# Moving a tile's scatter to the next tile's last unit, and a first exponential ahead of the loop

## The chip, the cores and the metric

The kernel runs on one core of a Trainium2 chip. The time is device microseconds of one launch. The engines are named as the profile names them: PE is TensorE (PEld its weight loads), DVE is VectorE, ACT is ScalarE, POOL is GpSimd, SP is SyncE. Each engine works through its own instructions in order; engines wait for each other by semaphores. A DMA is issued by the queue of one engine and carried out by 16 DMA engines that the core has.

## What is computed

One layer of graph attention over 3327 nodes with 1024 features each, with a residual:

```python
h = jnp.maximum(_layernorm(x, axis=-1), 0.0)
f = h @ Wf + bf
g = h @ Wg + bg
e = jax.nn.relu(f @ g.T)
scores = jnp.where(adj > 0, e, NEG)
attention = jax.nn.softmax(scores, axis=1)
out = x + attention @ (h @ W + bW)
```

The adjacency matrix `adj` (3327 x 3327, int32) is symmetric, has ones on its diagonal and few others: each row has some 17 neighbours on average. Rows of `attention` are zero away from those neighbours.

## The kernel before

The kernel uses that sparsity. A dense path (lines 38 to 292) stands ready for other inputs and is not run here. `edge_path` (from line 296) has two stages.

**First stage** (lines 354 to 671, up to about 250 us). It runs over 26 tiles of 128 rows. For each tile SP loads the adjacency rows `r` (line 410) and the rows of x (412); ScalarE turns the adjacency into 0 and 1 and counts them (420); POOL multiplies by the column number (427); VectorE takes the largest eight of each of 16 segments (478) and from these the list of the row's neighbours. Beside it x is normalised: mean and variance on VectorE for odd tiles (436) and on ScalarE for even ones (450, 453), a square root on ScalarE (446, 454), a reciprocal on VectorE (458), then scale and relu on ScalarE (463, 464). The normalised rows go to a table `hd` in HBM (466), the candidates to `cd` (471), the lists to `pd` (508). TensorE meanwhile transposes rows of Wg and Wf (534), ScalarE copies them out of PSUM (535), and TensorE multiplies them to one matrix A (554, 558), so that a score is h A h' plus a bias term. It also counts by degree (498, 503, with VectorE at 500), from which the nodes are sorted into 26 tiles of falling degree: `perm`.

**Edge stage** (from line 674). A tile s now holds 128 nodes of about the same degree; `CAPS[s]` says how many neighbours its nodes may have (37 for the first, 11 for the last). `ORDER` begins with tile 24, then 0 to 23, then 25. For a tile:

- `fetch` gathers by indirect DMA its lists `pi` and its own rows (744, 746; all gathers are issued at line 691 by POOL).
- `prepare` transposes the rows (703, 704) and multiplies them by A (764); `emptied` copies the result q out of PSUM (780) and refills the bank with the bias (727).
- `dots` gathers, for each neighbour k, 128 rows of `hd` into a buffer G (821; 26 buffers) and takes their dot products with q on VectorE (824).
- `softmax` (853 to 873) masks the scores, takes their maximum, and has ScalarE's exponential (860).
- `combine` sums the G rows by their weights. Some are scaled on ScalarE (904) and summed in PSUM by transposing matmuls (887), the others are added on VectorE (910).
- `project` multiplies the sum by W (918, 924). `result` copies it to a tile `res` (942; two buffers) and adds the rows of x to it by an accumulating gather (949).
- `finish` scatters `res` to the rows of the output (954). It is issued after the last gather traced so far (953).

A tile with more than 16 neighbours is split into two units, each with its own dots, softmax and combine; the others are one unit. Tiles 0 to 14 have two. The loop at line 1003 runs over the units. In a unit it fetches the tile after next (if the unit is its tile's last), takes the dots of the unit, its softmax, the first three dots of the next unit (`AHEAD`), finishes a waiting scatter (1013), combines, and in a tile's last unit issues the result of the tile before (1021) and prepares the tile after next.

What is traced in this order is then placed by a scheduler, which plans each engine's order from its own estimate of the durations. `in_line` and `tc.issue_after` tie single instructions to others. So a line moved or added can change the planned order elsewhere.

Of the kernel before, what the change touches and what calls it, by code (L numbers as in the profile page):

```python
# [8 lines left out]
FP = mybir.dt.float32  # L9
I32 = mybir.dt.int32  # L10
AF = mybir.ActivationFunctionType
# [284 lines left out]
def edge_path(ctx: ExitStack, tc: tile.TileContext, x, adj, Wf, bf, Wg, bg, W, bW, out, flag):  # L296
# [11 lines left out]
    nc = tc.nc  # L308
    N, D = x.shape
    O = W.shape[1]  # L310
    P = 128
# [26 lines left out]
    ident = const.tile([P, P], FP, name="ident")  # L338
# [345 lines left out]
    small = ctx.enter_context(tc.tile_pool(name="small", bufs=2))  # L684
# [36 lines left out]
    def filled(pool, name, row, w, at):  # L721
        ps = pool.tile([P, CB], FP, name=name)
        if at < 2:
            nc.tensor.matmul(ps, ident, A_sb[:, 0, :CB], start=True, stop=True)
        o = at * w % row.shape[1]
        banks[name, at] = ps
        return nc.scalar.copy(ps[:, :w], row[:, o : o + w])

    for at in range(2):
        filled(p_q, "ps_q", vb, QB, at)  # L730
        filled(p_o, "ps_o", bWb, CB, at)

    def fetch(s):

        if s == ORDER[1]:

            with tc.issue_after(st["gathered"].ins):
                return fetched(s)
        fetched(s)
# [8 lines left out]
    def prepare(s):  # L748
        e = st[s]
        pi = e["pi"]  # L750
        hT = hTpool.tile([P, KD, P], FP, name="hT")
        with in_line():
            copied, ins = transposed2(hT, e["hp"])
        if queue:
            queue["act"], queue["pe"] = copied, ins
        e["q"] = qpool.tile([P, QW], FP, name="q")
        e["ps_q"] = []
        for i, o in enumerate(range(0, QW, QB)):
            at = 3 * ORDER.index(s) + i
            ps = banks.pop(("ps_q", at))  # L760
            e["ps_q"].append(ps)
            with in_line():
                for k in range(KD):
                    ins = nc.tensor.matmul(  # L764
                        ps[:, :QB], hT[:, k, :], A_sb[:, k, o : o + QB], start=False, stop=(k == KD - 1),
                        skip_group_check=True,
                    )
            if queue:
                queue["pe"] = ins

            if not i:
                emptied(s, i)
        if not queue:
            prepared(s)
# [74 lines left out]
    def softmax(s, k0, k1, last):  # L849

        e = st[s]
        sc = e["sc"][:, k0:k1]
        nc.vector.scalar_tensor_tensor(sc, sc, 0.0, e["mask"][:, k0:k1], op0=ALU.max, op1=ALU.add)
        nm = small.tile([P, 1], FP, name="nm")
        nc.vector.tensor_reduce(nm, sc, AX.X, ALU.max, negate=True)
        if k0:
            nc.vector.tensor_tensor(nm, nm, e["nm"], op=ALU.min)  # L857
        l = small.tile([P, 1], FP, name="l")
        with in_line():
            nc.scalar.activation(sc, sc, AF.Exp, bias=nm, accum_out=l)  # L860
        if k0:
            al = small.tile([P, 1], FP, name="al")
            nc.scalar.activation(al, e["nm"], AF.Exp, bias=nm, scale=-1.0)
            nc.vector.scalar_tensor_tensor(l, e["l"], al, l, op0=ALU.mult, op1=ALU.add)
        if last:
            rs = small.tile([P, 1], FP, name="rs")
            nc.vector.reciprocal(rs, l)
            if k0:
                nc.vector.tensor_tensor(al, al, rs, op=ALU.mult)
            nc.vector.tensor_scalar(sc, sc, rs, None, op0=ALU.mult)  # L870
        if k0:
            queue["act"] = nc.scalar.activation(e["y"], e["y"], AF.Copy, scale=al)
        e["nm"], e["l"] = nm, l
# [19 lines left out]
    def combine(s, k0, k1, last):  # L893
        e = st[s]
        if not k0:
            e["y"] = G[s, 0]
        y = e["y"]
        e["first"] = True
        pe = on_tensor(s, k0, k1) if last else []
        for k in range(k0, k1):  # L900
            p = e["sc"][:, k : k + 1]
            g = G[s, k]
            if k in pe:
                queue["act"] = nc.scalar.activation(g, g, AF.Copy, scale=p)  # L904
                queue["pe"] = sum_transposed(e, g, e["first"], False)
                e["first"] = False
            elif k == 0:
                queue["act"] = nc.scalar.activation(y, y, AF.Copy, scale=p)  # L908
            else:
                e["summed"] = nc.vector.scalar_tensor_tensor(y, g, p, y, op0=ALU.mult, op1=ALU.add)  # L910

    def project(s):
        e = st[s]
        yT = yTpool.tile([P, KD, P], FP, name="yT")
        with in_line():
            queue["pe"] = sum_transposed(e, e["y"], e["first"], True)
            for g in range(0, KD, 4):
                queue["act"] = nc.scalar.copy(yT[:, g : g + 4, :], e["yT"][:, g : g + 4, :])  # L918
        e["o"] = []
        for o in range(OH):  # L920
            ps = banks.pop(("ps_o", OH * ORDER.index(s) + o))
            with in_line():
                for k in range(KD):
                    ins = nc.tensor.matmul(  # L924
                        ps, yT[:, k, :], W_sb[:, k, o * CB : (o + 1) * CB], start=False, stop=(k == KD - 1),
                        skip_group_check=True,
                    )
            e["o"].append(ps)
            queue["pe"] = ins

    def result(s):

        e = st[s]
        r = e["r"] = xpool.tile([P, O], FP, name="res")
        for o in range(OH):
            to, ps = r[:, o * CB : (o + 1) * CB], e["o"][o]
            if s == NT - 1:
                nc.vector.tensor_tensor(to, ps, e["x"][:, o * CB : (o + 1) * CB], op=ALU.add)
                continue
            at = OH * ORDER.index(s) + o + 2  # L940
            with in_line():
                ins = nc.scalar.copy(to, ps)  # L942
                if at < OH * NT:
                    ins = filled(p_o, "ps_o", bWb, CB, at)
            queue["act"] = ins


        if s < NT - 1:
            gather(r, x[:, :], perm[:, s : s + 1], compute_op=ALU.add)

    def finish(s):

        with tc.issue_after(st["gathered"].ins):
            ins = nc.gpsimd.indirect_dma_start(  # L954
                out=out[:, :],
                out_offset=bass.IndirectOffsetOnAxis(ap=perm[:, s : s + 1] if s < N // P else final, axis=0),
                in_=st[s]["r"],
                in_offset=None,
                bounds_check=None if s < N // P else N - 1,
                oob_is_err=s < N // P,  # L960
            )
        tc.declare_no_dep(ins.ins, group="results", reason="other rows")
        tc.add_to_no_dep_group("results", ins.ins)
# [19 lines left out]
    def dots(s, ks):  # L983
        for k in ks:
            if (s, k) not in done:
                done.add((s, k))

                dot(s, k, st[ORDER[-2]].get("summed") if s == ORDER[-1] else None)
# [13 lines left out]
    rest, done_with = None, []  # L1002
    for i, (s, k0, k1) in enumerate(units):
        last = k1 == CAPS[s]
        at = ORDER.index(s)
        if last and at + 2 < NT:
            fetch(ORDER[at + 2])
        dots(s, range(k0, k1))
        softmax(s, k0, k1, last)
        if i + 1 < len(units):  # L1010
            s2, a, b = units[i + 1]
            dots(s2, range(a, min(b, a + AHEAD)))
        if done_with:
            finish(done_with.pop())
        combine(s, k0, k1, last)
        if rest:
            rest()
            rest = None
        if last:
            if at:  # L1020
                result(ORDER[at - 1])
                done_with.append(ORDER[at - 1])
            if at + 2 < NT:
                prepare(ORDER[at + 2])

            def rest(s=s, at=at):
                if at + 2 < NT:
                    prepared(ORDER[at + 2])
                project(s)

            if not at or i + 1 == len(units) or units[i + 1][2] == CAPS[units[i + 1][0]]:
                rest()
                rest = None
            if at + 2 == NT - 1:
                bad = failed()
# [43 lines left out]
```

## Time and profile before

| | us |
|---|---|
| median of 7 runs | 1327.37 |
| lowest and highest of them | 1325.80, 1328.97 |
| profiled execution | 1324.11 |
| its span | 1322.4 |
| POOL, indirect DMA to G at line 691, 454 of them | 535.2 busy |
| VectorE, dots at line 824, 456 of them | 584.7 busy |
| VectorE, sums at line 910, 279 of them | 357.8 busy |
| TensorE, line 924, 832 matmuls | 365.7 busy |
| TensorE, line 764, 1248 matmuls | 368.0 busy |
| POOL idle ahead of the scatters at line 954 | 58.0 for res from DMA |

A row of a timeline below reads: start in us, duration in us, engine, line, operation, what is written from what, count, and in brackets the idle time of that engine just before it and what ended it. A row of waits reads: engine, what was to run, its line, whom it waited for, then us in all, times, and the longest. A row of windows has, for each stretch, the busy us of PE, PEld, DVE, ACT and POOL (instructions in parentheses), then TensorE's granted clock as a share of the full one, the busy share of the 16 DMA engines, and the GB/s.

### The profile page before, as it was taken

How to read it: one execution, taken by the hardware profiler on the slowest of the kernel's cores; microseconds unless marked ns; L12 is line 12 of the kernel's file. 1: busy time of each engine (PE TensorE's matmuls, PEld its weight loads, DVE VectorE, ACT ScalarE, POOL GpSimd, SP SyncE). 2: the span in 40 equal slices, each digit the busy share in tenths (PEclk: the TensorE clock that was granted, in tenths of full speed). 3: DMA queues.
4: the chain of work that ended last, by engine and by line, in shares of the span. 5: the costliest groups of instructions: out<-in, count | busy, mean ns of one | idle time of the engine just before them, and what ended most of it. 6: DMA issues, size and time to landing. Idle time of an engine off the chain costs nothing.

```text
span 1322.4 us, 14333 instructions
## 1 busy us (share of the span) xinstructions
PE 1113.7 (84%) x4448; PEld 706.3 (53%) x4448; DVE 1165.3 (88%) x2360; ACT 597.8 (45%) x940; POOL 896.2 (68%) x678
## 2 busy tenths in 40 slices
PE   2589797289329689899999998999999999999995
PEld 2355564156126547665666664666665555555553
DVE  4779899759977888999999999999989999999980
ACT  6779787214034525453454454334443333333350
POOL 6689889275556667777776777766666777776611
PEclk9999798589759899899999999999999999999998
DMA  9999996698458788889889889988887988888821
GB/s 351 338 368 355 386 370 243 233 320 321 152 182 307 271 298 266 297 308 309 312 294 313 313 307 320 306 263 300 279 287 245 294 284 289 275 270 281 285 85 50
DMA packets 101660, 374.46 MB, mean 283 GB/s; under 512 B 14731, under 2 KB 18474, under 8 KB 98247
## 3 DMA queue, kind: packets, MB, share of 16 engines
q0 software_dynamic: 79584, 286.77, 64.3%
q1 hardware_dynamic: 11004, 71.01, 14.0%
q10 hardware_dynamic: 10986, 15.67, 3.3%
q8 instruction: 37, 0.61, 0.2%
q14 instruction: 49, 0.40, 0.1%
HBM read 344.11 MB, written 29.30 MB: 282 GB/s over the span
## 4 chain that ended last, share of the span: by engine, by line
PE 35%; DVE 22%; issue 15%; ACT 10%; DMA 10%; POOL 7%; POOLq 0%; ACTq 0%; SPq 0%; DVEq 0%
PE ps_o L924 16%; PE ps_q L764 12%; DVE G L910 8%; ACT G L904 6%; DVE junk L824 6%; DMA G<-hd,pi 4%; DVE cand L478 4%; PE ps_A L554 4%; POOL G L691 3%; PE yT_ps L887 3%; POOL r L427 2%; DMA cd<-cand 1%; DMA res<-in_x_dram,perm 1%; ACT r L420 1%; DVE sc L824 1%
## 5 line engine op out<-in xcount | busy, mean ns | idle before, releaser
L691 POOL DMA_INDIRECT G<-hd,pi x454 | 535.2, 1179 | 199.3 <-issue 100.7
L824 DVE CUSTOM_DVE_ANT_0 junk<-G,q 128x1024 bf16<-128x1024 f32 x456 | 584.7, 1282 | 49.3 <-DMA G<-hd,pi 28.0
L924 PE MATMUL ps_o<-W_sb,yT 128*128 128x512 f32 x832 | 365.7, 597 | 21.8 <-ACT yT L918 21.8
L764 PE MATMUL ps_q<-A_sb,hT 128*128 128x342 f32 x1248 | 368.0, 454 | 8.7 <-ACT hT L704 8.7
L910 DVE SCALAR_TENSOR_TENSOR G<-G,sc 128x1024 f32<-128x1024 f32 x279 | 357.8, 1283 | 4.6 <-ACT G L908 3.9
L764 PEld LDWEIGHTS ps_q<-A_sb,hT 128*128 128x128 f32 x1248 | 234.9, 190 | 133.8 <-ACT hT L704 14.9
L924 PEld LDWEIGHTS ps_o<-W_sb,yT 128*128 128x128 f32 x832 | 155.6, 189 | 216.5 <-issue 188.4
L887 PE MATMUL yT_ps<-ident,G 128*128 128x128 f32 x1512 | 187.5, 283 | 72.7 <-ACT G L904 72.7
L887 PEld LDWEIGHTS yT_ps<-ident,G 128*128 128x128 f32 x1512 | 177.3, 146 | 98.5 <-ACT G L904 82.8
L427 POOL TENSOR_TENSOR r<-r,iotaj 128x1664 f32<-128x1664 f32 (+3 forms) x52 | 191.3, 3709 | 31.3 <-ACT r L420 26.8
L904 ACT ACTIVATE G<-G,sc 128x1024 f32<-128x1024 f32 x163 | 173.2, 1135 | 53.1 <-DVE sc L870 53.1
L780 ACT COPY q<-ps_q 128x342 f32<-128x342 f32 x78 | 34.7, 445 | 271.2 <-PE ps_q L764 271.2
L478 DVE MAX8 cand<-r 128x8 f32<-128x208 f32 (+2 forms) x416 | 121.8, 360 | 30.1 <-POOL r L427 30.1
L554 PE MATMUL ps_A<-WgT,WfT 128*128 128x342 f32 x432 | 141.9, 489 | 0.2 <-ACT WfT L535 0.2
L554 PEld LDWEIGHTS ps_A<-WgT,WfT 128*128 128x128 f32 x432 | 87.1, 207 | 59.8 <-issue 18.2
L420 ACT ACTIVATE r<-r 128x3327 f32<-128x3327 int32 (+4 forms) x28 | 77.8, 2780 | 1.4 <-ACT xt L464 0.5
L954 POOL DMA_INDIRECT out_dram<-res,perm x25 | 30.3, 1213 | 59.5 <-DMA res<-in_x_dram,perm 58.0
L860 ACT ACTIVATE sc<-sc,nm 128x10 f32<-128x10 f32 (+11 forms) x41 | 12.6, 308 | 120.6 <-DVE nm L857 110.7
L691 POOL DMA_INDIRECT res<-in_x_dram,perm x25 | 43.9, 1756 | 34.1 <-ACT res L942 28.9
L691 POOL DMA_INDIRECT pi<-pd,perm x26 | 29.8, 1146 | 39.2 <-issue 34.2
L942 ACT COPY res<-ps_o 128x512 f32<-128x512 f32 x50 | 28.7, 575 | 54.5 <-PE ps_o L924 54.5
L704 ACT COPY hT<-ps_t 128x512 f32<-128x512 f32 x52 | 28.0, 588 | 41.3 <-PE ps_t L703 41.2
(133 smaller groups left out, 685.1 us busy)
## 6 DMA issues: line engine op xcount, KB each, us to landing
r<-in_adj_dram SPq DMA_DIRECT2D x25, 1663.5 KB, 10.3
xt<-in_x_dram SPq DMA_DIRECT2D x25, 512.0 KB, 8.8
hd<-xt ACTq DMA_DIRECT2D x25, 512.0 KB, 8.5
G<-hd,pi POOLq DMA_INDIRECT x454, 6.1
wr<-in_L_gnn_Wg_dram SPq DMA_DIRECT2D x8, 512.0 KB, 6.4
wr<-in_L_gnn_Wf_dram SPq DMA_DIRECT2D x8, 512.0 KB, 7.3
W_sb<-in_L_gnn_W_dram SPq DMA_DIRECT2D x1, 4096.0 KB, 18.0
cd<-cand ACTq DMA_DIRECT2D x25, 64.0 KB, 8.5
```

The lines of the kernel that those rows point to most:

```text
L420: nc.scalar.activation(r[:n, b:e], a[:n, b:e], AF.Sign, accum_out=to)
L427: nc.gpsimd.tensor_mul(r[:n, b:e], r[:n, b:e], iotaj[:n, : e - b])
L478: nc.vector.max(cand[:n, s * 8 : s * 8 + 8], r[:n, s * SW : min(N, (s + 1) * SW)])
L554: nc.tensor.matmul(ps[:, :QB], WfTs[c][:, k, :], WgT[:, k, o : o + QB], start=(k == 0), stop=(k == KD - 1))
L691: return nc.gpsimd.indirect_dma_start(out=to, out_offset=None, in_=table, in_offset=bass.IndirectOffsetOnAxis(ap=idx, axis=0), **kw,)
L764: ins = nc.tensor.matmul(ps[:, :QB], hT[:, k, :], A_sb[:, k, o : o + QB], start=False, stop=(k == KD - 1), skip_group_check=True,)
L780: ins = nc.scalar.copy(e["q"][:, i * QB : (i + 1) * QB], e["ps_q"][i][:, :QB])
L824: nc.vector.tensor_tensor_reduce(junk, g, e["q"][:, :D], 1.0, e["q"][:, D : D + 1], op0=ALU.mult, op1=ALU.add, accum_out=e["sc"][:, k : k ...
L887: ins = nc.tensor.matmul(e["yT"][:, c, :], g[:, c * P : (c + 1) * P], ident, is_transpose=True, start=(first and c % 4 == 0), stop=(last a ...
L904: queue["act"] = nc.scalar.activation(g, g, AF.Copy, scale=p)
L910: e["summed"] = nc.vector.scalar_tensor_tensor(y, g, p, y, op0=ALU.mult, op1=ALU.add)
L924: ins = nc.tensor.matmul(ps, yT[:, k, :], W_sb[:, k, o * CB : (o + 1) * CB], start=False, stop=(k == KD - 1), skip_group_check=True,)
```

## The change

The scatter of a tile that waits to be finished is traced only in units that are the last of their tile, instead of in the next unit whatever it is. For tiles of one unit nothing changes. And before the edge stage's banks are filled, one activation with the exponential is added, on a single column, whose result nobody reads.

```diff
@@ -726,6 +726,10 @@
         banks[name, at] = ps
         return nc.scalar.copy(ps[:, :w], row[:, o : o + w])
 
+
+    one = small.tile([P, 1], FP, name="one")
+    nc.scalar.activation(one, ident[:, :1], AF.Exp)
+
     for at in range(2):
         filled(p_q, "ps_q", vb, QB, at)
         filled(p_o, "ps_o", bWb, CB, at)
@@ -1010,7 +1014,7 @@
         if i + 1 < len(units):
             s2, a, b = units[i + 1]
             dots(s2, range(a, min(b, a + AHEAD)))
-        if done_with:
+        if done_with and last:
             finish(done_with.pop())
         combine(s, k0, k1, last)
         if rest:
```

Line numbers in the text are those of the kernel before; in the changed kernel, lines from 728 on stand four further down.

## The prediction, made before the result was known

> **What bounds the kernel now.** I read the busy shares first, then cut the span into its stages, then read, stage by stage, which wait ends last there.
>
> The table by stage of core 0 (each engine's busy us, the granted clock, the share of the 16 DMA engines, GB/s):
>
> ```profile
> 0.00:250.00 250.00, 173.53 (x620) 113.85 (x620) 202.82 (x856) 183.33 (x276) 198.11 (x103) 0.91 0.91 344
> 250.00:400.00 150.00, 84.18 (x381) 57.59 (x381) 119.85 (x240) 40.41 (x61) 89.46 (x74) 0.77 0.67 232
> 400.00:600.00 200.00, 173.44 (x784) 117.89 (x783) 177.51 (x277) 90.99 (x136) 141.45 (x116) 0.94 0.86 290
> 600.00:950.00 350.00, 334.06 (x1377) 210.87 (x1376) 345.29 (x536) 157.36 (x257) 243.24 (x210) 0.99 0.88 302
> 950.00:1322.40 372.40, 348.48 (x1293) 206.10 (x1291) 319.87 (x456) 125.71 (x211) 223.97 (x177) 0.99 0.74 242
> ```
>
> The third busy number is VectorE. From 600 to 950 us it is busy 345.3 of 350, so no earlier gather can help there. From 950 on TensorE is the bound, and that stretch ends in the last tiles, each of one unit. Only 400 to 600 leaves VectorE idle in the part that the moved scatter touches: 22.5 of 200 us. Before 250 the engines hand tiles to each other, with the DMA engines 0.91 busy.
>
> What VectorE waits for from 400 to 650, and what the scatters (line 954) wait for there:
>
> ```profile
> DVE junk L824 <- DMA G<-hd,pi: 22.0, 20, 2.7
> ...
> POOL out_dram L954 <- DMA res<-in_x_dram,perm: 17.8, 6, 4.2
> ```
>
> POOL stands 17.8 us at six scatters; VectorE waits 22.0 us for gathered rows. These are not the same microseconds. One tile in order of time, first POOL, then VectorE:
>
> ```profile
> 460.40 1.59 POOL L691 DMA_INDIRECT res<-in_x_dram,perm  x1 [0.30 <-ACT ps_o L727]
> 462.29 1.86 POOL L691 DMA_INDIRECT G<-hd,pi  x1 [0.30 <-issue]
> 464.46 0.95 POOL L691 DMA_INDIRECT G<-hd,pi  x1 [0.30 <-issue]
> 469.28 1.00 POOL L954 DMA_INDIRECT out_dram<-res,perm  x1 [3.86 <-DMA res<-in_x_dram,perm]
> 470.58 1.41 POOL L691 DMA_INDIRECT G<-hd,pi  x1 [0.30 <-issue]
> ```
>
> ```profile
> 469.87 1.29 DVE L824 CUSTOM_DVE_ANT_0 junk<-G,q 128x1024 bf16<-128x1024 f32 x1 [2.68 <-DMA G<-hd,pi]
> ...
> 472.41 2.60 DVE L910 SCALAR_TENSOR_TENSOR G<-G,sc 128x1024 f32<-128x1024 f32 x2
> 475.42 1.28 DVE L824 CUSTOM_DVE_ANT_0 junk<-G,q 128x1024 bf16<-128x1024 f32 x1 [0.41 <-DMA G<-hd,pi]
> ```
>
> The gather-add of x into res (460.40) has not landed, so the scatter holds POOL's queue 3.86 us, and every gather behind it. The 2.68 us wait at 469.87 is for a row issued ahead of the scatter: moving the scatter does nothing to it. The row issued behind the scatter (470.58) costs VectorE only 0.41 us, because two weighted sums (line 910, 2.60 us) lie between.
>
> **Scatter part.** With two-unit tiles the scatter is traced one unit later. In the built order 11 scatters move back: from 2 gathers after their res gather to 12, 9, 7, 7, 7, 4, 6, 5, 5, 3 and 3. Nothing is added; each is one POOL issue (1.0 us, 0.3 between) with its DMA, moved past 1 to 10 gathers, ahead of the next fetch of pi as before, and past nothing of SP's. For the first five a gather costs about 1.25 us (0.95 plus 0.30), so 7 of them take 8.75 us behind the 1.9 us of the res issue: 10.6 us. The row above shows res landed 8.6 us after its issue (469.0 against 460.4). So those scatters no longer wait, and the gathers behind come 3.86 + 1.3 us earlier in this tile. The price of the later scatter is 1.3 us of POOL, beside line 910; without that cover it would be at most 1.3 us a tile.
>
> What VectorE gets back are only the waits on rows issued behind a scatter. In order of time these are 0.31 (420.44), 0.41 (475.42), 1.17 (527.65), 0.71 (569.71) and 0.94 us (609.26): 3.54 us. The other 18.5 us stand ahead of the scatter in their tile. A lead won by POOL is not carried into the next tile: it waits for free G buffers before each tile ends (4.9 us for line 910 at 446). Below 600 us everything that follows waits on VectorE, which has 1.3% idle there, so the 3.54 us should pass to the end. Bounds: 0 (the rows are late anyway) and 6 (some of the 18.5 goes too, because a row ahead of it has less traffic beside it).
>
> A rule speaks against it. The Trainium skill, "DMA: Bandwidth & Descriptors", section "Issuing engines are not separate DMA queues", says that transfers from all queues share the same 16 DMA engines and interleave; then a POOL freed sooner wins nothing while these are full. The windows around the stall:
>
> ```profile
> 466.00:468.00 2.00, 2.00 (x9) 1.31 (x8) 1.19 (x2) 1.92 (x4) 0.00 (x0) 1.00 1.00 289
> 468.00:470.00 2.00, 2.00 (x9) 1.31 (x8) 0.13 (x1) 0.00 (x0) 0.72 (x1) 1.00 0.72 295
> 470.00:472.00 2.00, 2.00 (x9) 1.31 (x8) 1.96 (x3) 0.89 (x2) 1.68 (x2) 1.00 0.63 256
> 472.00:474.00 2.00, 2.00 (x9) 1.31 (x8) 1.96 (x4) 0.00 (x0) 1.40 (x2) 1.00 0.65 152
> ```
>
> Up to 468 the DMA engines are full (share 1.00) and the rule holds. Then they drain: 0.28, 0.37 and 0.35 of three windows of 2 us are 2.0 us unused. By the rule alone the gain is 0; by the row up to 2.0 us per tile can be filled, more than any of the five waits. I take 3.5.
>
> **Exponential part.** ScalarE's table is loaded three times now, the last time here:
>
> ```profile
> 298.04 1.28 ACT L860 ACT_TABLE_LOAD   x1
> 299.81 0.30 ACT L860 ACTIVATE sc<-sc,nm 128x12 f32<-128x12 f32 x1 [0.49 <-DVE nm L855]
> ```
>
> The Trainium skill, "ScalarE: Activation LUTs", section "What ACT_TABLE_LOAD costs", prices a change of set at about 2.66 us (1.28 load and 1.38 drain). Had the change removed this load, that price would give −2.66. The row gives 0: after the load ScalarE waits 0.49 us more for nm from VectorE. And it is not removed. The new activation depends only on ident, so the scheduler puts it first on ScalarE; the square root of the first stage then changes the set, and the load ahead of line 860 is still there: three loads in both. The new activation itself (estimate 0.3 us, from line 454's 0.29) and its load stand before ScalarE's first work, line 450 at 9.14, which waits 7.05 us for its x tile: that idle time hides them. What it does cost is order: the first stage is planned anew. On ScalarE two copies of WgT (line 535), at 21.00 and 21.85 now, come behind lines 463 and 464, where ScalarE waits for VectorE until 25.79:
>
> ```profile
> 25.79 0.29 ACT L463 ACTIVATE nmr<-nmr,rstd 128x1 f32<-128x1 f32 x1 [3.35 <-DVE rstd L458]
> ...
> 28.76 2.98 ACT L420 ACTIVATE r<-r 128x3327 f32<-128x3327 int32 x1 [0.45 <-DVE cand L478]
> ```
>
> Those copies empty the banks for the next eight transposes, so these start near 27.8 instead of 22.5, and the last copy ends near 30.4 (27.8, two lots of four transposes at 1.0, a copy at 0.6). The cd store and then line 420 follow at 30.85: 2.1 us later than 28.76. POOL waits for exactly that (it starts tile 2 at 31.91 after 2.51 us idle), and the chain of waits runs through this line 420. Behind it stand VectorE's maxima of tile 2 and the next line 463. On SP a row of Wg and the load of r for tile 3 (24.82) slip by some 5 us, but line 420 needs that tile at 42.21, and it has landed about 10 us after its issue; behind the SP wait only loads stand.
>
> Against this, TensorE's order gets better near 91 us: it stood 4.75 us there at line 503 for VectorE, and now has ten matmuls of line 554 between. That frees up to 1.7 us, the time that ScalarE's line 535 then waits for TensorE at 110.93. A hd store near 88.6 goes behind a line 420 (3.4 us later); the loads behind it have about that slack. I take +1.5, near the row of line 420 less a third for TensorE. Bounds: −3 and +6.3 (all of the copies' delay, 21.0 to 27.3, reaching the end of the stage).
>
> **Sum.** −3.5 + 1.5 = −2.0 us. The profiled execution took 1324.11 us (1322.4 span and 1.7 around it), 3.3 below the median of the seven runs; the same difference on the median gives 1327.37 − 2.0 = 1325.4 us. A difference of 0.2% is 2.65 us, about what a measurement of this kernel can tell from no change.
>
> **Rivals.**
> The first stage comes out even or better (TensorE's filled stall counts, the slip is caught up by loads running ahead): −3.5 to −6, so 1321.4 to 1323.9. For it: the DMA engines have 9% free up to 250, and tiles are buffered five deep. Against: the chain of waits runs through the line 420 that slips.
> The gather gain doesn't come: full DMA engines deliver the rows when they did before. Then +1.5 remains, 1328.9, within the bound; the drained windows speak against it.
> Slower: the displaced WgT copies alone. They hold TensorE's transposes, SP's row of Wg and behind it all loads, with the DMA engines at 1.01 before and dry after 25 us. If the whole 6.3 us reaches the end of the stage, the time is 1327.37 − 3.5 + 6.3 = 1330.2. It decides from a loss of 3.5 us on, and measurably from 6.2. For it: loads have 0.91 of the DMA engines up to 250 and lost time there isn't made up if they bound it. Against: VectorE, not loads, is what runs almost without idle from 100 to 136 us.
>
> **How the numbers follow.** The likeliest case (−2.0, spread ±1.5) has 0.40: two thirds within 0.2%, one third faster. The better first stage has 0.26, all faster. No gather gain has 0.14, mostly same, a quarter slower. The slip or another mischief of the new order has 0.20, all but a tenth slower. Faster 0.13 + 0.26 = 0.39; slower 0.18 + 0.04 = 0.22; same 0.39. The range: the better case reaches to 1321.4 and the slip to 1330.2; 1320.5 to 1330.5 leaves out the rarer sums of both.
>
> **What would show it.** The waits of line 954 on res should fall from 58.0 us to about 25 in all and to near 0 from 400 to 650; VectorE's waits for G there from 22.0 to about 18.5; the table loads stay three, one of them at line 860; the first line 824 of the edge stage and line 427's third tile start 1 to 2 us later. Wrong would be: VectorE's waits ahead of the scatters shrink as well, or the first stage ends more than 4 us away from its old place.

## The result, and the profile after

The changed kernel takes 1321.86 us (median of 15 runs, 1319.82 to 1325.99); the kernel before, over 36 runs, 1327.44 us. The ratio is 0.9961, with a 95% interval of 0.9951 to 0.9971: 5.2 us less (3.8 to 6.5). Its profiled execution took 1320.29 us, with a span of 1318.6 against 1322.4. Differences in us, here and below, are worked out from the ratio, not from the two medians. Six of the runs further down (they are marked) were made on chips where the kernel before itself takes 1341 to 1357 us and its times spread widely, so that their ratios have wide intervals; a ratio leaves out executions more than 1.5% above the fastest of the same kernel, the medians do not.

The table by stage of the changed kernel, columns as before:

```profile
0.00:250.00 250.00, 169.83 (x620) 111.12 (x620) 202.12 (x856) 182.38 (x277) 198.02 (x103) 0.93 0.91 344
250.00:400.00 150.00, 84.08 (x383) 57.24 (x382) 120.68 (x241) 40.39 (x61) 88.65 (x75) 0.78 0.67 232
400.00:600.00 200.00, 175.50 (x791) 116.92 (x789) 178.35 (x281) 92.49 (x141) 148.37 (x117) 0.96 0.88 294
600.00:950.00 350.00, 334.64 (x1387) 212.34 (x1385) 346.50 (x537) 155.91 (x253) 251.01 (x212) 0.99 0.89 302
950.00:1318.60 368.60, 344.68 (x1276) 203.49 (x1274) 316.15 (x449) 125.64 (x211) 219.81 (x174) 0.99 0.74 242
```

VectorE's work by 400 us is about the same (322.8 us against 322.7); from 400 to 950 it gets 2.0 us more done. POOL is busy 14.7 us longer from 400 to 950 us, but with only 3 instructions more (329 against 326): the single gather takes longer (1212 ns on average against 1179 over the whole kernel), so this is not work won.

Waits from 400 to 650 us, first VectorE's, then POOL's:

```profile
DVE junk L828 <- DMA G<-hd,pi: 20.8, 16, 2.8
...
POOL G L691 <- DVE G L914: 16.9, 16, 4.9
...
POOL out_dram L958 <- issue: 2.0, 6, 0.5
```

The line for free buffers in the kernel before:

```profile
POOL G L691 <- DVE G L910: 7.6, 5, 4.9
```

The six scatters (now line 958) stand no longer for res: 17.8 us are gone from POOL. But POOL stands 9.3 us longer (16.9 against 7.6) for free G buffers behind the sums of line 914 (910 before), and VectorE's wait for rows falls only from 22.0 to 20.8 us.

The same tile as in the prediction, POOL and then VectorE:

```profile
462.38 2.25 POOL L691 DMA_INDIRECT res<-in_x_dram,perm  x1 [0.30 <-ACT hT L704]
464.94 0.97 POOL L691 DMA_INDIRECT G<-hd,pi  x1 [0.31 <-issue]
466.22 1.65 POOL L691 DMA_INDIRECT G<-hd,pi  x1 [0.30 <-issue]
468.18 1.01 POOL L691 DMA_INDIRECT G<-hd,pi  x1 [0.30 <-issue]
...
479.72 0.99 POOL L958 DMA_INDIRECT out_dram<-res,perm  x1 [0.31 <-issue]
```

```profile
465.76 1.28 DVE L828 CUSTOM_DVE_ANT_0 junk<-G,q 128x1024 bf16<-128x1024 f32 x1 [1.25 <-DMA G<-hd,pi]
471.17 1.28 DVE L828 CUSTOM_DVE_ANT_0 junk<-G,q 128x1024 bf16<-128x1024 f32 x1 [2.79 <-DMA G<-hd,pi]
```

The gathers follow one another without the 3.86 us hole, and the scatter issues without a wait. The short wait behind the scatter (0.41 us) is gone; the long one ahead of it, for a row issued just behind the gather-add of x, is still there, 2.79 us against 2.68. The DMA engines are no longer dry in this place:

```profile
468.00:470.00 2.00, 2.00 (x9) 1.31 (x8) 0.38 (x2) 1.70 (x4) 1.52 (x2) 1.00 0.97 320
470.00:472.00 2.00, 2.00 (x9) 1.31 (x8) 0.83 (x1) 0.10 (x1) 1.39 (x3) 1.00 1.00 360
472.00:474.00 2.00, 2.00 (x8) 1.32 (x7) 1.95 (x5) 0.80 (x2) 1.70 (x2) 1.00 1.02 395
```

Shares of 0.97 to 1.02 (a packet counts in the window in which it starts, so a share can pass 1), where the kernel before had 0.72, 0.63 and 0.65.

Where the time is won shows best when the k-th dot product (line 824, in the changed kernel 828) is set beside the k-th of the other trace. Starts in us, worked out from the timelines of four kernels, two of which belong to the experiments below. Each shift is against the column to its left: `after` against `before`, `scat_only` (the moved scatters alone) against `exp_only` (the scatters in their old place):

```
   k   before   after (shift)     exp_only  scat_only (shift)
   0   304.41   304.88 (+0.47)     304.71   303.75 (-0.96)
 102   514.77   515.49 (+0.72)     514.78   514.63 (-0.15)
 126   566.49   565.03 (-1.46)     568.09   565.09 (-3.00)
 150   617.99   614.43 (-3.56)     620.89   614.80 (-6.09)
 168   651.25   647.68 (-3.57)     655.43   648.00 (-7.43)
 300   929.25   925.44 (-3.81)     933.43   925.80 (-7.63)
 450  1270.65  1266.85 (-3.80)    1274.84  1267.18 (-7.66)
```

Nothing is won up to 515 us, which takes in the first two of the tiles with a stall at the scatter. Everything is won between 515 and 655 us, and it stays until the end. Each column is one execution: beside `before` in place of `exp_only`, `scat_only` leads by 3.5 us at k = 450, not by 7.7.

The exponential, on ScalarE:

```profile
296.78 1.28 ACT L864 ACT_TABLE_LOAD   x1
300.28 0.30 ACT L864 ACTIVATE sc<-sc,nm 128x12 f32<-128x12 f32 x1 [2.22 <-DVE nm L859]
```

There are three table loads as before, one still ahead of this line, and behind it ScalarE waits for VectorE. In the first stage the step forecast for the new order is there, ScalarE first, then POOL:

```profile
26.16 0.30 ACT L463 ACTIVATE nmr<-nmr,rstd 128x1 f32<-128x1 f32 x1 [5.28 <-DVE rstd L458]
...
30.74 2.98 ACT L420 ACTIVATE r<-r 128x3327 f32<-128x3327 int32 x1
...
33.88 7.36 POOL L427 TENSOR_TENSOR r<-r,iotaj 128x1664 f32<-128x1664 f32 x2 [4.11 <-ACT r L420]
...
47.33 3.71 POOL L427 TENSOR_TENSOR r<-r,iotaj 128x1664 f32<-128x1664 f32 x1 [6.08 <-ACT r L420]
```

Line 420 starts at 30.74 (28.76 before), POOL's tiles at 33.88 and 47.33, each 2.0 us later. But the stage ends only 0.25 us later (VectorE's line 621 at 246.78 against 246.53). VectorE's wait for TensorE in the first 250 us, before and after, shrank by 3.5 us, which is one place that can have taken the slip up:

```profile
DVE hit L500 <- PE pre L498: 5.7, 7, 4.2
```

```profile
DVE hit L500 <- PE pre L498: 2.2, 5, 1.1
```

### The profile page after: what moved, and what is told of

The parts are those of the page before. It is cut to its first block, busy times and chain, and to the rows that moved or that the text cites. A ratio compares the mean times of both kernels' runs of the same rounds, so it can differ in the third digit from the quotient of the medians.

```text
span 1318.6 us, 14342 instructions
## 1 busy us (share of the span) xinstructions
PE 1108.7 (84%) x4448; PEld 701.1 (53%) x4448; DVE 1163.8 (88%) x2360; ACT 596.8 (45%) x941; POOL 905.9 (69%) x678
## 4 chain that ended last, share of the span: by engine, by line
PE 37%; DVE 21%; issue 16%; POOL 9%; DMA 9%; ACT 7%; POOLq 0%; ACTq 0%; DVEq 0%; SPq 0%
PE ps_o L928 16%; PE ps_q L768 12%; DVE G L914 8%; POOL r L427 6%; DVE junk L828 5%; DMA G<-hd,pi 5%; PE yT_ps L891 5%; ACT G L908 4%; DVE cand L478 3%; PE ps_A L554 3%; POOL G L691 3%; DMA G<-hd,perm 1%; DVE sc L828 1%; DMA hd<-xt 1%; ACT hT L704 1%
## 5 line engine op out<-in xcount | busy, mean ns | idle before, releaser
L691 POOL DMA_INDIRECT G<-hd,pi x454 | 550.5, 1212 | 209.7 <-issue 89.2
L427 POOL TENSOR_TENSOR r<-r,iotaj 128x1664 f32<-128x1664 f32 (+3 forms) x52 | 191.2, 3707 | 30.9 <-ACT r L420 30.5
L554 PE MATMUL ps_A<-WgT,WfT 128*128 128x342 f32 x432 | 137.7, 477 | 2.8 <-ACT WfT L535 2.8
L554 PEld LDWEIGHTS ps_A<-WgT,WfT 128*128 128x128 f32 x432 | 84.4, 200 | 61.9 <-issue 21.4
L958 POOL DMA_INDIRECT out_dram<-res,perm x25 | 28.0, 1121 | 36.8 <-DMA res<-in_x_dram,perm 32.3
L534 PE MATMUL ps_tr<-ident,wr 128*128 128x128 f32 x128 | 25.7, 360 | 25.2 <-DMA wr<-in_L_gnn_Wg_dram 13.4
```

Of the source, the lines that this page charges most:

```text
L427: nc.gpsimd.tensor_mul(r[:n, b:e], r[:n, b:e], iotaj[:n, : e - b])
L554: nc.tensor.matmul(ps[:, :QB], WfTs[c][:, k, :], WgT[:, k, o : o + QB], start=(k == 0), stop=(k == KD - 1))
L691: return nc.gpsimd.indirect_dma_start(out=to, out_offset=None, in_=table, in_offset=bass.IndirectOffsetOnAxis(ap=idx, axis=0), **kw,)
```

## The experiments

Theory: the moved scatters alone make the gain, by the waits for rows gathered behind a scatter that stood; the exponential saves no load and only re-plans the first stage. Rivals: the exponential has a share; what a tile loses is not the wait at the scatter but the gather-add ahead of the rows, or the bytes of either.

### The two parts, each alone

`exp_only` has the activation and not the scatter's condition; `scat_only` the reverse:

```diff
-        if done_with:
+        if done_with and last:
             finish(done_with.pop())
```

> The exponential activation alone, scatters as before. My theory, from the two traces: it takes away no table load (three stay, the last one at line 860) and only re-plans the first stage, whose end moved by 0.25 to 0.47 us; so -0.5 to +1.0 us against the kernel before, no difference. Rival: the exponential part holds a share of the 5.6 us that the two medians differ by (the loads come earlier, the new order of the first stage is better): then -2 us or more. By the price of a table load and its drain alone -2.66.

Measured: 1328.99 us (22 runs) against 1326.81 (27 runs of the kernel before), ratio 1.0012 (1.0002 to 1.0023): +1.6 us (0.3 to 3.1). The rival is out; the part costs a little. The theory's −0.5 to +1.0 lies below the middle of the interval, its upper end within it.

> The moved scatters alone, no exponential activation. My theory: all of the gain is here. The two traces give -4.3 us behind the first stage (the first product of line 824 starts 0.47 us later and the last ones 3.80 us earlier), so -4 to -5.5 us against the kernel before, and VectorE's products fall ahead in the three tiles between 515 and 610 us. Rival: only a part is here, -2 to -3 us, and the rest is the exponential's.

Measured: 1320.47 us (6 runs), ratio 0.9948 (0.9929 to 0.9967): −6.9 us (−9.4 to −4.4). All of the gain is here, and more than the whole change shows; it is larger than the theory's −4 to −5.5, whose range lies within the interval only in part. The two ratios multiply to 0.9960; both parts together measured 0.9961.

The trace of `exp_only` is a second look at the scatters in their old place, in an execution of 1328.2 us, nearer to the median than the first profile's 1324.1. One tile of it, POOL's scatter and VectorE's waits for rows behind two scatters:

```profile
605.11 1.76 POOL L954 DMA_INDIRECT out_dram<-res,perm  x1 [3.59 <-DMA res<-in_x_dram,perm]
```

```profile
571.31 1.28 DVE L824 CUSTOM_DVE_ANT_0 junk<-G,q 128x1024 bf16<-128x1024 f32 x1 [0.71 <-DMA G<-hd,pi]
...
612.03 1.28 DVE L824 CUSTOM_DVE_ANT_0 junk<-G,q 128x1024 bf16<-128x1024 f32 x1 [1.95 <-DMA G<-hd,pi]
...
655.43 1.29 DVE L824 CUSTOM_DVE_ANT_0 junk<-G,q 128x1024 bf16<-128x1024 f32 x1 [0.91 <-DMA G<-hd,pi]
```

The waits behind its six scatters are 0.25, 0.24, 1.40, 0.71, 1.95 and 0.91, together 5.46 us; the first profile had 3.54 over five tiles and none in the sixth. From 515 to 660 us VectorE waits 11.5 us for rows in `exp_only` and 4.9 in `scat_only`: 6.6 less, 5.0 of it behind the scatters. From 400 to 515 us it waits 14.3 and 17.0: 2.7 more. So in the first tiles more comes back as longer waits ahead of the scatters than is won behind them (0.5 us). How much of the 6.9 us these waits explain hangs on the execution that is taken for the kernel before: in the first profile they are 7.3 us from 515 to 660 and 14.6 from 400 to 515, and beside it `scat_only` is 2.4 us better and 2.4 worse.

### The table loaded where ScalarE is idle

`exp_late` is the changed kernel with another operand, which exists only at the end of the first stage:

```diff
-    nc.scalar.activation(one, ident[:, :1], AF.Exp)
+    nc.scalar.activation(one, bads[:, 2:3], AF.Exp)
```

> As the changed kernel, but the exponential activation reads a value that the first stage ends with, so that the order of the first stage stays as before and ScalarE's table for the exponential is loaded near 268 us, where ScalarE is idle, and not at 297 us ahead of line 864. This does what the change's words say. My theory: the time is that of the moved scatters alone, within 1 us, because behind the load line 864 waited for nm from VectorE anyway (2.22 us in the changed kernel's profile, 0.49 in the one before). Rival: the load lay on the path and 1.3 us (the load) to 2.7 us (load and drain, by the page) are gained on top.

Measured: 1320.68 us (6 runs), ratio 0.9949 (0.9930 to 0.9967), 0.2 us from `scat_only` on the same chip. The table loads (a list of groups: count, busy us and mean ns, idle before) and the first exponential:

```profile
L731 ACT ACT_TABLE_LOAD x1 | 1.3, 1283 | 0.0
```

```profile
301.33 0.30 ACT L864 ACTIVATE sc<-sc,nm 128x12 f32<-128x12 f32 x1 [3.29 <-DVE nm L859]
```

The load is gone from line 864, and the wait for nm is 3.29 us in place of 2.22 behind the load: ScalarE waits longer for the same operand. A load with a wait behind it was worth nothing. This trace says something on the first stage too: line 621 stands at 248.1 us, 2.0 us later than in `scat_only` (246.1; why is not known, since the order of the first stage was meant to stay), and the spans are equal, 1318.9. The dot products are 2.2 us apart at k = 0 and 0.1 us at k = 150. In this pair of traces a slip of 2 us at the end of the first stage is absorbed in the stretch that waits for rows.

### The gather-add and its place

If a row ahead of the scatter is late because the gather-add of x stands in front of it on POOL, that one is to be moved. `add_later` issues it behind the tile's last row and scatters in the next tile's first unit; `added` holds the gather of line 949:

```diff
+        if last and to_add and CAPS[s] > ONE_CHUNK:
+            added(to_add[-1])
+            done_with.append(to_add.pop())
         softmax(s, k0, k1, last)
...
-        if done_with:
+        if done_with and (not last or CAPS[s] <= ONE_CHUNK):
             finish(done_with.pop())
...
-                done_with.append(ORDER[at - 1])
+                if i + 1 < len(units) and CAPS[units[i + 1][0]] > ONE_CHUNK:
+                    to_add.append(ORDER[at - 1])
+                else:
+                    added(ORDER[at - 1])
+                    done_with.append(ORDER[at - 1])
```

> The gather-add of x into res is issued behind the tile's last gathered row in its second unit, where before it stood at the head of the tile, and the scatter follows in the next tile's first unit; no exponential activation. My theory: the 18 to 20 us that VectorE still waits from 400 to 650 us are for rows that stand behind this gather-add on POOL's queue (1.9 us of issue a tile, and 0.5 MB beside the rows); moved behind the last row it delays none of them. So -5 to -10 us against the kernel before, more than the moved scatters give. Rival: those rows wait for free buffers or for DMA engines that are full, whatever is issued ahead of them: then no better than the moved scatters, -4 us, or worse, because the gather-add now delays the next tile's first rows and pi.

Measured: 1312.42 us (6 runs), ratio 0.9894 (0.9874 to 0.9914): −14.1 us (−16.7 to −11.4), twice the moved scatters' gain. This form leaves out the scatter of one tile (tile 12). Its lead is there long before that scatter's turn, which comes near 930 us: the dot products stand 14.0 us earlier than before at k = 150 and 13.6 at k = 450. But 2.7 us of it are there at k = 0, ahead of all these tiles (line 621 stands at 243.8 us in this trace, 246.5 before), and have another cause. The tile near 460 us on POOL, VectorE's waits from 400 to 650, and the stage from 400 to 600:

```profile
459.31 1.16 POOL L691 DMA_INDIRECT G<-hd,pi  x1 [0.30 <-issue]
460.77 1.02 POOL L691 DMA_INDIRECT G<-hd,pi  x1 [0.30 <-issue]
462.10 1.03 POOL L691 DMA_INDIRECT G<-hd,pi  x1 [0.30 <-DMA G<-hd,pi]
463.43 1.68 POOL L691 DMA_INDIRECT res<-in_x_dram,perm  x1 [0.30 <-issue]
```

```profile
DVE junk L824 <- DMA G<-hd,pi: 12.0, 9, 3.6
```

```profile
400.00:600.00 200.00, 181.81 (x803) 120.35 (x802) 186.24 (x288) 93.02 (x144) 150.28 (x121) 0.97 0.91 307
```

In this tile six rows that stood behind the gather-add now stand ahead of it (it follows the 85th gathered row of the loop, before the 79th; three of the six are shown). VectorE waits 12.0 us where it waited 22.0, and does 8.7 us more work from 400 to 600 us. If each wait is put down to the place of its row on POOL's queue (the k-th gathered row belongs to the k-th dot product), the rows issued within 5 us behind a gather-add, ahead of any scatter, cost VectorE 9.8 us from 400 to 665 us in the kernel before, 8.9 in the changed kernel and nothing here. That is about what the waits fall by from the changed kernel to this one, 20.8 to 12.0.

`add_later2` is the same with every scatter issued, measured on a chip of the other kind; `add_later3` is the same kernel again, on another such chip:

```diff
-        if done_with and (not last or CAPS[s] <= ONE_CHUNK):
-            finish(done_with.pop())
+        while done_with and (not last or CAPS[s] <= ONE_CHUNK):
+            finish(done_with.pop(0))
```

> The gather-add of x behind the tile's last gathered row, with every tile's scatter issued (the first form of it left the last two-unit tile's scatter out). My theory: one scatter is 1.3 us of POOL among some 900, in a stretch where VectorE or TensorE is the bound, so the time is that of the first form within 1.5 us: 1312 to 1315 us, -12 to -15 against the kernel before. Rival: the missing scatter was a part of that gain; then -8 to -11.

> The same kernel as the complete form of the moved gather-add. Where that one ran, the traces show TensorE, VectorE and ScalarE standing some 50 us in all with nothing to wait for (put down as issue), in the kernel before too, which the first profiles do not show; its ratio of 0.9946 is blurred by them. My theory: where they are absent it gains what its first form did, ratio 0.988 to 0.991. Rival: the ratio stays at 0.994 to 0.996, because the scatter that the first form left out was worth the rest.

Measured: ratio 0.9946 (0.9918 to 0.9974) and 0.9972 (0.9948 to 0.9996), where the kernel before took 1346.4 and 1356.9 us. In us that is −7.3 (−11.0 to −3.5) and −3.8 (−7.1 to −0.5). The complete form is faster than the kernel before on both, but by these runs not shown to be faster than the changed kernel, and the gain of its first form has not been repeated with it: both theories missed; the first rival's −8 to −11 us lies within its interval, the second's 0.994 to 0.996 in part within its own. Traces of these chips show why they are blurred (last section). What the move was made for is there all the same: VectorE's waits for rows from 400 to 650 us in `add_later2` and `add_later3`, where the kernel before on such a chip (`before_again`, below) has 24.8.

```profile
DVE junk L824 <- DMA G<-hd,pi: 17.5, 15, 3.4
```

```profile
DVE junk L824 <- DMA G<-hd,pi: 12.1, 12, 3.0
```

But stalls that hold VectorE back also give rows more time to land, so these two lines alone prove no gain.

### What of the gather-add costs

`no_add2` leaves the gather-add out where the scatter falls in a two-unit tile, with the scatters in their old place; x is missing from those outputs. `scat_sp2` has the moved scatters, and in two-unit tiles a plain load of 128 rows of x over res from SP's queue:

```diff
-        if s < NT - 1:
+        if s < NT - 1 and CAPS[ORDER[ORDER.index(s) + 2 if ORDER.index(s) + 2 < NT else -1]] <= ONE_CHUNK:
             gather(r, x[:, :], perm[:, s : s + 1], compute_op=ALU.add)
```

```diff
-            gather(r, x[:, :], perm[:, s : s + 1], compute_op=ALU.add)
+            nc.sync.dma_start(out=r, in_=x[s * P : (s + 1) * P, :]) if CAPS[s] > ONE_CHUNK else gather(r, x[:, :], perm[:, s : s + 1], compute_op=ALU.add)
```

> The gather-add left out again for tiles whose scatter falls in a two-unit tile (x is missing from the output there), scatters where they were. The first run of it fell where ScalarE, TensorE and VectorE stand for some 50 us with nothing that the trace shows, in every kernel. My theory: where that is absent, it gains -13 to -17 us, because it takes away both the wait at the scatter (6 us) and the gather-add ahead of the rows (8 us). Rival A: -6 us, the wait alone. Rival B: the first run's +4.6 us is its own, and repeats: then the gather-add and its wait cost nothing, and the gain of the moved scatters has another cause.

> The moved scatters with the gather-add of x on POOL replaced by a plain load of x into res from SP's queue in the two-unit tiles (the sum of x and the product is left out there), once more. Theory A: what the gather-add at the head of a tile costs is POOL's issue ahead of the rows, 1.9 us in each of some five tiles: -8 us against the moved scatters alone, near 1312, ratio 0.988 to 0.990. Theory B: its bytes beside the rows are the cost: near 1320, ratio 0.994 to 0.996. The first run's 1.0071 fell among the stalls that no wait explains.

Measured: `no_add2` 1313.52 us against 1327.83, ratio 0.9882 (0.9860 to 0.9904), −15.7 us. `scat_sp2` 1314.94 against 1326.83, ratio 0.9907 (0.9892 to 0.9923), −12.3 us. VectorE's waits for rows from 400 to 650 us, first of `no_add2`, then of `scat_sp2`:

```profile
DVE junk L824 <- DMA G<-hd,pi: 14.7, 16, 2.0
```

```profile
DVE junk L824 <- DMA G<-hd,pi: 15.7, 17, 2.7
```

Without the gather-add, a scatter in its old place loses nothing (0.3 to 0.4 us ahead of each of the six from 400 to 650 us): the wait was the gather-add's, as theory had it, and leaving it out is worth as much as moving both, within the intervals. With SP's load in place of it, 5.4 us are won over the moved scatters alone (12.3 less 6.9, on two chips, with 2 to 2.5 us either way on each) although as many bytes of x are read. The ratio of 0.9907 lies between the ranges of the two theories, nearer to A (POOL's issue, 0.988 to 0.990) than to B (0.994 to 0.996). It isn't proof for the issue alone: the plain load differs from the gather-add in that it reads whole rows in order and does not read res. What is left to `no_add2`, 3.4 us, lies within the intervals.

The first runs of these two, and two more, fell on the chip of `add_later2`; `before_again`, the kernel before unchanged, on a third such chip:

> As the kernel before, scatters where they were, but the gather-add of x is left out for every tile whose scatter falls in a two-unit tile; x is missing from the output there. The scatter then waits for nothing but ScalarE's copy. My theory: it takes away the wait of the scatter (the 6 us of the moved scatters) and the gather-add's own cost at the head of the tile (the 8 us more of the moved gather-add): -13 to -17 us, as good as moving both. Rival: what the moved gather-add gained came from its new place beside the scatter and not from the head of the tile: then -6 us.

> The moved scatters (no exponential activation), and in the two-unit tiles the gather-add of x on POOL replaced by a plain load of 128 rows of x into res from SP's queue, in the same place: as many bytes read, the same wait for ScalarE's copy, but 1.9 us less of POOL per tile. It leaves out the sum of x and the product in those tiles, since the load overwrites res. Theory A: what the gather-add at the head of a tile costs is POOL's issue time ahead of the rows: 1.9 us in each of some five tiles, so -8 us against the moved scatters alone, near 1312. Theory B: its cost is its bytes beside the rows of G on the DMA engines: then within 2 us of the moved scatters alone, near 1320.

> As the kernel before, but the scatters that fall in two-unit tiles are left out; those rows of the output are missing. My theory: a scatter that waits for nothing is free (1.3 us of POOL beside VectorE's sums), so this gives what moving them gave, -5 to -8 us. Rival: the 0.5 MB that each writes, and its issue, compete with the rows of G: then -9 us or more, and moving the scatter leaves something to gain.

> The kernel before, unchanged, for a second profile. The first profiled execution took 1324.1 us, 3.3 below the median, and the sum of my prediction was read from its waits. My theory: the execution-to-execution spread lies in VectorE's waits for rows between 400 and 660 us, so a profile nearer to the median (1326 to 1329 us) shows 25 us or more of them against 22.0 from 400 to 650, and 5 us or more on rows issued behind a scatter against 3.54. Rival: the spread lies in the first stage or the end, and the waits are the same 22 and 3.5 us.

Measured: `no_add` 1349.19, ratio 1.0034 (1.0002 to 1.0065); `scat_sp` 1353.56, 1.0071 (1.0037 to 1.0105). Both are slower there and 1% faster on the other chips: the sign of this edit hangs on the chip. `no_scatter` (`finish` left out in two-unit tiles, and with it those rows of the output) took 1330.41, ratio 0.9895 (0.9842 to 0.9949): −14.1 us with an interval of −21 to −7, which theory's −5 to −8 touches and the rival's −9 or more covers. But its trace does not show this gain where either looked for it. VectorE's waits for rows from 400 to 650 us:

```profile
DVE junk L824 <- DMA G<-hd,pi: 24.1, 14, 4.1
```

That is about as much as in `before_again` (24.8) and in the first profile (22.0): there is no scatter to wait behind, but the rows issued within 5 us behind a gather-add cost 15.5 us in place of 9.8. Beside the first profile its dot products are 3.0 us late at k = 0, 3.8 at k = 168 and 6.7 at k = 450; those of `before_again` 5.1, 6.3 and 17.0. What sets these two traces apart comes mostly behind k = 168, where VectorE hardly waits for rows any more. So the run decides nothing between theory and rival, and it leaves a doubt: in this trace a queue that never stops at a scatter did not by itself shorten the waits for rows.

`before_again` took 1341.0 us beside 1351.0 of a second execution of the same kernel, with 24.8 us of waits for rows, of which 3.4 us are behind scatters: near the theory's 25 in the first, the rival's 3.5 in the second. A chip with stalls answers little on the 1324 to 1329 us that the run was meant for, and `exp_only`'s trace has to stand in for it.

## Why the prediction was right or wrong

- **Time.** Forecast 1325.4, measured 1321.9, inside the range and faster by more than 0.2%. It lies where the rival with an even or better first stage put it, but not by that cause: the exponential part cost what was forecast, and the scatter part gained twice as much. That the time fell into the range is in part luck: the larger term was half of what was measured, and the smaller one came out without the slip that it was worked out from.
- **POOL's waits.** "From 58.0 us to about 25 in all and to near 0 from 400 to 650": 32.3 in all, and none for res there. Right.
- **The scatter's −3.5.** The mechanism holds from 515 us on, where the waits behind scatters (2.8 us in the first profile, 5.0 in `exp_only`) are gone in both traces with moved scatters; in the two tiles before, it won nothing. The size was wrong: −6.9 (−9.4 to −4.4) measured alone. The term mis-sized is the sum of the waits behind the scatters. It was read from one execution, and one that the prediction itself noted as 3.3 us below the median; a difference to the median was then added as a constant. But the slower execution of `exp_only` lies behind it in part by this term: 5.46 us against 3.54, with a sixth tile. Its dot products are 0.3 us later than those of the first profile at k = 0, and 4.2 us at k = 168. So the term is not the same in each execution, and a sum read from one fast execution can be too small. That it grows with the time of the execution is not shown: `before_again` has 3.4 us of it at 1341 us. The rest of the −6.9 is not accounted for term by term.
- **"The other 18.5 us stand ahead of the scatter ... moving the scatter does nothing to it."** Wrong, in both directions. In the tiles at 400 and 450 us those waits grew from 13.1 to 16.0 us (from the two traces, before and after), which ate all that was won there. From 515 us on they shrank, from 4.5 us to 3.6, and from `exp_only` to `scat_only` from 6.5 to 4.9; the prediction had named this as a sign of being wrong. The upper bound of 6 us, given for this case, was near the truth. The forecast that VectorE's waits from 400 to 650 us fall from 22.0 to about 18.5 missed for the same reason: 20.8.
- **"A lead won by POOL is not carried into the next tile."** Mostly right: POOL's waits for buffers behind line 914 grew by 9.3 of the 17.8 us. That later tiles gained more than earlier ones is no proof against it; no run separates the two.
- **Rule and row on the DMA engines.** The row was right that they had room: the windows filled from 0.63 to 0.72 up to 0.97 to 1.02. The rule that the prediction took from the Trainium skill ("DMA: Bandwidth & Descriptors", section "Issuing engines are not separate DMA queues"), one set of DMA engines for all queues, has its share all the same: in that tile the row ahead still came late, 2.79 us. Filling the hole brought other rows sooner, not this one.
- **The exponential's +1.5.** Measured +1.6 (0.3 to 3.1). The size held, the way did not. Line 420 and POOL's tiles slipped by the 2.0 us forecast, but the part that TensorE and others took up, set at a third, was nearly all: 0.25 to 0.5 us reached line 621, and the first line 824 started 0.5 us later, where 1 to 2 had been forecast. VectorE's wait at line 500, 5.7 us before and 2.2 after, can have taken most of it up; and in `exp_late` even 2 us at the end of the stage didn't reach the end of the kernel. So the agreement of the number is luck. By which way `exp_only` then loses its 1.6 us stays open: its trace is late only in the waits from 515 to 655 us, and those vary between executions of one kernel.
- **The table load.** The row said 0; the price of the Trainium skill ("ScalarE: Activation LUTs", section "What ACT_TABLE_LOAD costs") said −2.66 us. `exp_late` takes the load away from line 864 and its median is 0.2 us above that of `scat_only`: no gain. The row was right, since the wait for nm lay behind the load. Of that price the traces show the load of 1.28 us but not the drain of 1.38: at line 454 in the kernel before, ScalarE's copy ends at 15.43 us, the load runs from 15.45 to 16.73, and the activation starts at 16.74.
- **The rival "slower".** The slip of the loads came, but it did not reach the end of the stage: from 26 to 32 us the DMA engines are 0.24, 0.64 and 0.41 busy in three windows of 2 us, where they had been 1.07, 1.03 and 0.99, and line 621 is 0.25 us later.

## What to carry to other kernels

A DMA that waits on a queue stops everything behind it, but its price is not its own wait (17.8 us here): it is the wait of the engine that ends last, for the things behind it (3.4 to 5.5 us in three executions with the scatters in their old place), and one execution is a thin base for it. When such a wait is found, look at what it waits for: moving or leaving out the gather-add that the scatter waited for gave twice what moving the scatter gave, since that also stood ahead of rows that were late. So far this is shown only by runs whose output lacks something (`add_later` the rows of one tile, `no_add2` x in 14 tiles); the complete form gained 3.8 and 7.3 us on chips with stalls and was not measured on another. Here a table load and a slip of 2 us, each with a wait behind it, were worth nothing; find the wait that takes such a term up before it is counted.

## What was not expected of the hardware

On the chips of `exp_only`, `no_add2` and `scat_sp2`, and in the measurement of the result, the kernel before took 1327 to 1328 us, on three others 1341 to 1357. On the latter, engines stand with their inputs ready. One place in `add_later2`, TensorE and then ScalarE:

```profile
513.59 1.04 PE L703 MATMUL ps_t<-ident,G 128*128 128x128 f32 x8
523.66 6.78 PE L764 MATMUL ps_q<-A_sb,hT 128*128 128x342 f32 x16 [9.03 <-issue]
```

```profile
512.96 0.59 ACT L727 COPY ps_o<-bWb 128x512 f32<-128x512 f32 x1
523.02 0.59 ACT L704 COPY hT<-ps_t 128x512 f32<-128x512 f32 x1 [9.47 <-remote]
```

The transposes that ScalarE's copy needs end at 514.63, ScalarE has been free since 513.55, and the copy starts at 523.02: 8.4 us in which nothing in the trace holds it, and TensorE waits with it. From 250 to 1310 us ScalarE stands 51.7 us at this line with such an unknown releaser in `add_later3`, 34.3 in `add_later2`, 30.9 in `scat_sp`, 26.4 in `no_add`, 13.2 in `no_scatter` and 6.7 in `before_again`; in the traces of the other chips there is none. Why they come is not known. One trace of each kernel cannot say whether some kernels draw more of them than others; but a gain measured on these chips can be a difference in these stalls.
